# Moving loads, grouping the tails of two norms, and lending one weighting to POOL in a four-layer graph network kernel

## The chip, the cores and the metric

The kernel runs on one NeuronCore of a Trainium2 chip. The core has five engines with a queue each: PE (TensorE, matmuls; its weight loads are listed as PEld), DVE (VectorE), ACT (ScalarE), POOL (GpSimd) and SP (SyncE, which here only issues transfers). Engines execute their queues in order and wait for each other through semaphores. Transfers run on 16 DMA engines that all queues share. The metric is the device time of one execution in microseconds (us). Before the change three runs gave 7698.37, 7705.21 and 7706.85 us; the median is 7705.21.

## What is computed

A stack of four graph layers over 6250 nodes with 128 features and 100000 edges, sorted by their target `dst`. Each layer works on `h = relu(layernorm(x))` and adds its result to `x`. Shortened from the reference:

```python
# layer 0: attention summed into the source nodes, one softmax over all edges
h = h @ W_w + W_b
e = leaky_relu(h[src] @ a_src + h[dst] @ a_dst + a_b, 0.01)
out = segment_sum(softmax(e, axis=0) * h[dst], src)
# layer 1: message network, mean over dst, node network
m = relu(concat(h[src], edge_attr) @ W1a + b1a) @ W1b + b1b
agg = segment_sum(m, dst) / clip(count(dst), 1)
out = relu(concat(h, agg, u[0]) @ W2a + b2a) @ W2b + b2b
# layer 2: two graph attentions, four heads and one, each with batch norm and PReLU
h1 = prelu(bn(gatv2(h, heads=4)), pa)
h2 = prelu(bn(gatv2(h1, heads=1)), pa)
out = h2 + h @ skipW + skipb
# layer 3: three edge convolutions
for conv in (in, hid, out):
    z = relu(concat(h[dst], h[src] - h[dst]) @ W1 + b1) @ W2 + b2
    h = segment_max(z, dst)      # 0 where a node has no edge; relu between
```

All in float32, except some masks and counts in bfloat16.

## The kernel before

**Tiles.** Nodes are padded to 49 tiles of 128 (NT), edges to 782 tiles of 128 (TR), which are worked on in 196 chunks of 512. `x` stays on the chip as one tile of 128 x 49 x 128. What edges read of nodes is written as a table to memory, and POOL fetches its rows by indirect transfers, 128 rows each (`gather`, L390): the tables are T1 for layer 1 (`g`), TL1 and TL2 for layer 2's two attentions (`gl`, both named by their buffers `TL` and `TLb`), TB for each edge convolution (`gb`, three times 782). Layer 0 goes the other way: POOL scatters rows by source node into `rows_d` (`scatter`, L1259), a region per part, four parts in all, which SP clears ahead with `clear_rows` (L261).

**Preamble** (L116 to L255). `x` is loaded on ScalarE's queue in seven transfers of 448 KB. The edge lists `d_i` (SP) and `s_i` (ScalarE) are turned by VectorE and TensorE into columns of one number per edge. Then a loop over edge tiles counts how many edges each source tile has: VectorE compares (`oh`, L230), TensorE sums (`pc`, L233). Inside that loop the generator `node_steps` (L279) advances by one step per round. Its first steps load layer 0's weights (`wx`, `bx`, `av`), clear the rows of part 0 and append two columns to the weights, products with `av` (L308, L309); each later step does one node tile: normalise, transpose, project with `wx` and add the bias as a one-row product (L338, L339), copy to `ev` and store in the table T0 (L347). At the end a flag decides between the fast program, which runs here, and a general one.

**Layer 0's last part** (L1464 to L1550). When the last scatter is through, the rows of the fourth part are read back seven node tiles at a time. For each node tile ScalarE weights the J = 4 rows of each partition (`weigh`, L1301), VectorE builds a one-hot matrix (`oq`, L1303), TensorE sums (L1490), and the tile goes on to the layer norm of layer 1 and into T1.

**Mean layer, attentions.** The mean layer ends with the last node tile's network and the tables TL1 and TR1 (L1732, L1733). `attentions` (L1766) begins with the load of the single number `pa` (L381) and its negation `npa` (L1786). Each attention ends in `norm` (L2068): batch norm and PReLU of four node tiles at a time into `z`, then `finish` for every single tile: `to_tables` (L2124) projects to the second attention's tables TL2 and TR2; `to_x` (L2137) transposes, adds to `x`, layer-normalises, transposes and projects to the tables TA and TB of the first edge convolution, as three steps in a pipeline over tiles.

**Edge convolutions** (L2191). Per chunk TensorE builds the first layer's sum from TA and TB, ScalarE rectifies it (`z`, L2256), TensorE applies the second layer, VectorE scans for the running maximum. The first layer's bias is in the table TA by way of a row `bab` that `finish` (L2294) and `to_x` add.

**Order.** The Python code gives each engine's instructions; a scheduler sets their order per queue, so that an operation can stand earlier or later in its engine's queue than its line suggests.

Of the kernel before, what the change touches and what calls it, by code (L numbers as in the profile page):

```python
# [88 lines left out]
def tile_gnn_stack(ctx: ExitStack, tc: tile.TileContext, a: dict, out: bass.AP):  # L89
# [32 lines left out]
    xr = a["x"].rearrange("(i p) f -> p i f", p=P)  # L122
    for i in range(0, NT, 7):
        nc.scalar.dma_start(x[:, i:i + 7, :], xr[:, i:i + 7, :])
# [7 lines left out]
    with ExitStack() as st:  # L132
# [3 lines left out]
        node = node_steps(nc, tc, a, sh, st)  # L136
        d_i = one.tile([R, 1024], I32, name="d_i")
        nc.sync.dma_start(d_i, a["dst"].rearrange("(r j) -> r j", j=1024))
        s_i = one.tile([R, 1024], I32, name="s_i")
        nc.scalar.dma_start(s_i, a["src"].rearrange("(r j) -> r j", j=1024))  # L140
        edge_i = one.tile([R, 2], I32, name="edge_i")
# [137 lines left out]
def node_steps(nc, tc, a, sh, st):  # L279
# [3 lines left out]
    x, ident, ones = sh["x"], sh["ident"], sh["ones"]  # L283
# [3 lines left out]

    wx = one.tile([P, D + 2], F32, name="wx")
    bx = one.tile([1, D + 2], F32, name="bx")
    nc.scalar.dma_start(wx[:, :D], a["L0_gnn_W_w"])  # L290
    b0 = a["L0_gnn_W_b"]
    nc.scalar.dma_start(bx[:, :D], bass.AP(tensor=b0.tensor, offset=b0.offset, ap=[[0, 1], [1, D]]))
# [11 lines left out]
    clear_rows(nc, sh["rows_d"][0], none, 0)  # L304
    for j, av in enumerate(avs):
        for t, n in ((wx, P), (bx, 1)):
            pr = one.tile([n, D], F32, name=f"pr{n}")
            V.tensor_tensor(pr, t[:, :D], av[:n, :], OP.mult)  # L308
            V.tensor_reduce(t[:, D + j:D + j + 1], pr, AX.X, OP.add)  # L309
# [26 lines left out]
    def project(i):  # L336
        pp = ps.tile([P, D + 2], F32, name="np")
        nc.tensor.matmul(pp, live.pop(i), wx, start=True, stop=False)  # L338
        nc.tensor.matmul(pp, ones[0:1, :], bx, start=False, stop=True)  # L339
        live[i] = pp  # L340

    def keep(i):
        pp = live.pop(i)
        ev = w.tile([P, D + 1], F32, name="ev", bufs=4)
        S.copy(ev, pp[:, :D + 1])
        S.copy(sh["s_tab"][:, i:i + 1], pp[:, D + 1:])
        nc.sync.dma_start(sh["T0"][i * P:(i + 1) * P, :], ev)  # L347

    for i in range(NT + 2):
        if i < NT:  # L350
            norm(i)
        yield
        if 0 <= i - 1 < NT:
            project(i - 1)
        if 0 <= i - 2 < NT:
            keep(i - 2)
        yield
# [849 lines left out]
def attention_sum(ctx, tc, a, x, hT, T1, sh, ln_relu, transposed, bcast_row):  # L1207
# [89 lines left out]
    def weigh(w, rb, ew, J, row, bufs):  # L1297

        wt = w.tile([P, J, D], F32, name=f"wt{J}", bufs=bufs)
        for j in range(J):  # L1300
            S.activation(wt[:, j, :], rb[:, j, :D], AF.Copy, scale=ew[:, j:j + 1])  # L1301
# [182 lines left out]
    def total(b):  # L1484
        g, i = divmod(b, 7)
        ew, mv = accs[g]
        wt, oq = weigh(w, groups[g][:, i, :, :], ew[:, i, :], J, bank[:, P + 8:], 2)
# [278 lines left out]
def attentions(ctx, tc, a, x, TL1, TR1, TA, TB, sh, bcast_row, column, gather):  # L1766
# [17 lines left out]
    pa = bcast_row(cst, a["L2_gnn_pa"], 1, "pa")  # L1784
    npa = cst.tile([P, 1], F32, name="npa")
    V.tensor_scalar(npa, pa, -1.0, None, op0=OP.mult)  # L1786
# [281 lines left out]
    def norm(se, one, yT, stats, name, blocks, gam, bet, finish):  # L2068
# [14 lines left out]
        else:  # L2083
            eps = own.tile([P, 1], F32, name="leps")
            V.memset(eps, LN_EPS)
            wts.update(zip(("wab", "bab"), edge_weights(nc, own, a, "in")), eps=eps)
# [21 lines left out]
        for i0 in range(0, NT, 4):  # L2108
# [12 lines left out]
            for j in range(n):  # L2121
                finish(w, ps, i0 + j, z[:, :, j * P:(j + 1) * P])

    def to_tables(w, ps, i, z):  # L2124
        pp = ps.tile([P, 2 * D], F32, name="pp")
        for b in range(2):
            nc.tensor.matmul(pp, z[:, b, :], wts["wlr"][:, b, :], start=b == 0, stop=b == 1)
        ev = w.tile([P, 2, D + 1], F32, name="ev", bufs=4)
        V.tensor_tensor(ev[:, :, :D], pp.rearrange("p (s f) -> p s f", s=2),
                        wts["blr"].rearrange("p (s f) -> p s f", s=2), OP.add)  # L2130
        V.memset(ev[:, 0, D:], 1.0)
        nc.sync.dma_start(TL2[i * P:(i + 1) * P, :], ev[:, 0, :])
        nc.sync.dma_start(TR2[i * P:(i + 1) * P, :], ev[:, 1, :D])
# [3 lines left out]
    def to_x(w, ps, i, z):  # L2137
        n = slice(i * P, (i + 1) * P)
        it = {}

        def add():
            pp = ps.tile([P, P], F32, name="px")
            nc.tensor.transpose(pp, z[:, 0, :], ident)
            V.tensor_tensor(x[:, i, :], x[:, i, :], pp, OP.add)
            it["h"] = layer_norm(nc, w, x[:, i, :], wts["eps"])

        def turn():
            pp = ps.tile([P, P], F32, name="ph")
            nc.tensor.transpose(pp, it["h"], ident)
            it["hT"] = w.tile([P, P], F32, name="hT")  # L2150
            S.copy(it["hT"], pp)

        def tables():
            pp = ps.tile([P, 2 * D], F32, name="pp")
            nc.tensor.matmul(pp, it["hT"], wts["wab"], start=True, stop=True)
            ev = w.tile([P, 2 * D], F32, name="ev", bufs=4)
            V.tensor_tensor(ev, pp, wts["bab"], OP.add)  # L2157
            nc.sync.dma_start(TA[n, :], ev[:, :D])
            nc.sync.dma_start(TB[n, :], ev[:, D:])

        steps.append((add, turn, tables))
        for j in range(3):
            if i - j >= 0:
                steps[i - j][j]()
            if i == NT - 1:
                for m in range(j):
                    steps[i - m][j]()
# [7 lines left out]
def edge_weights(nc, pool, a, nm):  # L2175
# [7 lines left out]
    bab = pool.tile([P, 2 * D], F32, name=f"bab_{nm}")  # L2183
    V.memset(bab[:, D:], 0.0)
    b1 = a[f"L3_gnn_b1_{nm}"]
    nc.sync.dma_start(bab[:, :D], bass.AP(tensor=b1.tensor, offset=b1.offset, ap=[[0, P], [1, D]]))
    return wab, bab
# [3 lines left out]
def edge_convs(ctx, tc, a, x, TA0, TB0, hrow_d, sh, column, gather):  # L2191
# [21 lines left out]
    wab, bab, wo, bo = [None], [None], [], []  # L2213
# [154 lines left out]
```

## Time and profile before

| what | value |
|---|---|
| median of three runs | 7705.21 us |
| profiled execution | 7696.22 us |
| its span, first to last instruction | 7694.4 us |
| mean granted TensorE clock | 0.902 |
| busy: PE, DVE, ACT, POOL | 80%, 64%, 27%, 69% |
| indirect transfers on POOL: rows_d, g, gl (TL), gl (TLb), gb | 782 x 0.993, 782 x 0.947, 782 x 0.965, 782 x 1.002, 2346 x 0.957 us |

How to read it. The page shows the span in 40 slices of about 192 us; a digit is the busy share of a slice in tenths. Groups are instructions of one line, engine and shape with their busy time, the mean of one in ns, and the idle time of the engine before them with what ended it. In the timeline a line is: start, length, engine, line, operation, output<-input, and in brackets the idle time before and what ended it; a Q behind the engine's name marks the issue of transfers. From the timeline the stages are: preamble to about 172 us, layer 0's scattering parts to about 1204, its last part to 1322, mean layer to 2343, first attention to 3472 and its norm to 3537, second attention to about 4595 and its norm to 4674, edge convolutions to 7680, storing the output to 7694.

### The profile page before, as it was taken

To read this page: it belongs to the slowest core of one execution; us is meant where nothing else is said; L and a number is where in the kernel's file an instruction comes from. 1 tells how busy PE (TensorE), PEld (TensorE's weight loads), DVE (VectorE), ACT (ScalarE), POOL (GpSimd) and SP (SyncE) were. 2 spreads that over 40 slices of the span, in tenths; PEclk is the share of its full clock that TensorE was granted. 3 is DMA by queue.
4 is the path that set the end of the run, shared out by engine and by line. 5 is a ranking of instruction groups with operands and counts; after the bars stand their busy time and mean duration, and the time that the engine had idled before them with its cause. 6 is when DMAs were issued, how large, how long until landed. Compare 5 with 4: busy or idle time off the path is not lost.

```text
span 7694.4 us, 109942 instructions
## 1 busy us (share of the span) xinstructions
PE 6191.9 (80%) x35616; PEld 4418.6 (57%) x35616; DVE 4916.1 (64%) x15100; ACT 2115.0 (27%) x5081; POOL 5303.9 (69%) x5487
## 2 busy tenths in 40 slices
PE   6778886777777999996777777878778887777877
PEld 4677875555555666664554544555555555555554
DVE  5677886444446999995666666555555555555555
ACT  2134556222222222222111123222222222222222
POOL 0777772777776666654777755777767777677776
PEclk7778997999998999998888889999989999899999
DMA  3855763333336455433333324444434444333333
GB/s 121 258 162 168 216 189 124 93 92 93 92 87 133 142 144 146 143 104 95 88 89 93 89 79 125 122 126 122 126 114 123 125 122 126 110 119 118 117 118 108
DMA packets 778747, 954.40 MB, mean 124 GB/s; under 512 B 232584, under 2 KB 552494, under 8 KB 777942
## 3 DMA queue, kind: packets, MB, share of 16 engines
q1 hardware_dynamic: 555332, 519.06, 23.3%
q0 software_dynamic: 187680, 411.54, 18.5%
q10 hardware_dynamic: 35154, 16.67, 0.8%
q8 instruction: 289, 4.73, 0.3%
q14 instruction: 292, 2.39, 0.1%
HBM read 809.79 MB, written 137.02 MB: 123 GB/s over the span
## 4 chain that ended last, share of the span: by engine, by line
PE 39%; DMA 25%; POOL 13%; issue 9%; DVE 9%; ACT 2%; SPq 0%; POOLq 0%; DVEq 0%; ACTq 0%
DMA gb<-TB,srcE 13%; POOL gb L391 6%; PE pa L2011 5%; PE pz L2263 5%; DMA gl<-TLb,srcE 4%; PE pa L2290 4%; DMA g<-T,srcE 3%; PE pm L1892 3%; POOL gl L391 3%; DMA rows_d<-rw,pos 3%; PE pt L2251 3%; POOL g L391 3%; PE pb L2276 2%; PE pt L2253 2%; PE bank L1409 2%
## 5 line engine op out<-in xcount | busy, mean ns | idle before, releaser
L391 POOL DMA_INDIRECT gb<-TB,srcE x2346 | 2246.1, 957 | 859.6 <-issue 650.5
L2265 DVE TENSOR_TENSOR_SCAN sc<-mk,sc,pz 128x512 f32<-128x512 bf16 x585 | 748.4, 1279 | 1123.2 <-PE pz L2263 1123.2
L391 POOL DMA_INDIRECT gl<-TLb,srcE x782 | 783.5, 1002 | 364.4 <-issue 183.2
L391 POOL DMA_INDIRECT gl<-TL,srcE x782 | 754.4, 965 | 360.7 <-issue 153.8
L391 POOL DMA_INDIRECT g<-T,srcE x782 | 740.8, 947 | 357.5 <-issue 165.8
L2253 PE MATMUL pt<-ident,gb 128*128 128x128 f32 x2346 | 487.2, 295 | 608.0 <-DMA gb<-TB,srcE 597.3
L1259 POOL DMA_INDIRECT rows_d<-rw,pos x782 | 776.8, 993 | 251.8 <-issue 174.1
L2253 PEld LDWEIGHTS pt<-ident,gb 128*128 128x128 f32 x2346 | 315.2, 142 | 1051.8 <-DMA gb<-TB,srcE 772.9
L2256 ACT ACTIVATE z<-pt 128x512 f32<-128x512 f32 (+1 forms) x588 | 350.4, 596 | 1678.8 <-PE pt L2253 1571.3
L1897 ACT COPY mT<-pm 128x512 f32<-128x512 f32 (+1 forms) x588 | 343.7, 585 | 1399.0 <-PE pm L1894 1279.5
L1894 PEld LDWEIGHTS pm<-ident,gl 128*128 128x128 f32 x2346 | 317.9, 148 | 634.6 <-issue 318.2
L1892 PE MATMUL pm<-oh,wr 128*128 128x512 f32 (+1 forms) x1176 | 655.7, 641 | 31.6 <-DMA oh<-in_edge_weight 16.1
L2263 PE MATMUL pz<-z,wo 128*128 128x512 f32 (+1 forms) x1176 | 670.4, 655 | 0.0
L2290 PE MATMUL pa<-en,row 128*128 128x128 f32 x4692 | 669.0, 289 | 0.0
L2290 PEld LDWEIGHTS pa<-en,row 128*128 128x128 f32 x4692 | 624.2, 207 | 0.1
L1894 PE MATMUL pm<-ident,gl 128*128 128x128 f32 x2346 | 429.0, 290 | 239.9 <-DMA gl<-TLb,srcE 238.8
L2251 PE MATMUL pt<-oh,wr 128*128 128x512 f32 (+1 forms) x1176 | 612.5, 603 | 0.5 <-DVE ev L2157 0.5
L1898 DVE SCALAR_TENSOR_TENSOR lT<-mT,pm 128x512 f32<-128x512 f32 (+1 forms) x588 | 390.7, 675 | 286.1 <-ACT mT L1897 276.7
L2282 DVE TENSOR_SCALAR en<-iof,endE 128x128 f32<-128x128 f32 x2346 | 550.1, 301 | 0.0
L2276 PEld LDWEIGHTS pb<-ident,sc 128*128 128x128 f32 x2346 | 324.6, 153 | 357.9 <-issue 355.8
L2278 ACT COPY row<-pb 128x512 f32<-128x512 f32 (+1 forms) x588 | 344.1, 585 | 503.9 <-PE pb L2276 502.9
L2011 PE MATMUL pa<-px,oe 128*128 128x260 f32 x1564 | 407.7, 400 | 17.5 <-ACT px L2002 17.5
(346 smaller groups left out, 11735.5 us busy)
## 6 DMA issues: line engine op xcount, KB each, us to landing
mk<-mk_d SPq DMA_DIRECT2D x192, 1024.0 KB
mk<-mk_d SPq DMA_DIRECT2D x96, 512.0 KB
rows<-rows_d SPq DMA_DIRECT2D x98, 390.0 KB
gb<-TB,srcE POOLq DMA_INDIRECT x2346
wr<-TA SPq DMA_DIRECT2D x141, 256.0 KB
rows_d<-none SPq DMA_DIRECT2D x3, 9360.0 KB
ea<-in_edge_attr SPq DMA_DIRECT2D x195, 128.0 KB
wr<-TR SPq DMA_DIRECT2D x47, 448.0 KB
```

The costliest lines, as they stand in the source:

```text
L391: nc.gpsimd.indirect_dma_start(out=dst, out_offset=None, in_=table, in_offset=bass.IndirectOffsetOnAxis(ap=idx, axis=0),)
L1259: ins = nc.gpsimd.indirect_dma_start(out=rows_d[s], out_offset=bass.IndirectOffsetOnAxis(ap=idx, axis=0), in_=src, in_offset=None)
L1892: nc.tensor.matmul(pm[:, c0 * P:], wr[:, fb], oh[:, c0 * P:], start=True, stop=False)
L1894: nc.tensor.matmul(pm[:, c * P:(c + 1) * P], gl[:, c, fb], ident, start=False, stop=c == 3, is_transpose=True)
L2011: nc.tensor.matmul(pg, oe[:, c, :], px[:, c, :], start=c == c0, stop=c == 3)
L2251: nc.tensor.matmul(pt[:, c0 * P:], wr, oh[:, c0 * P:], start=True, stop=False)
L2253: nc.tensor.matmul(pt[:, c * P:(c + 1) * P], gb[:, c, :], ident, start=False, stop=c == 3, is_transpose=True)
L2263: nc.tensor.matmul(pz[:, c0:], wo[conv], z[:, c0:], start=True, stop=True)
L2265: V.tensor_tensor_scan(sc[:, c0:], masks.pop(k)[1][:, c0:], pz[:, c0:], 0.0 if carry[0] is None else carry[0][:, 511:512], OP.add, OP.max)
L2276: nc.tensor.transpose(pb[:, c, :], sc[:, c * P:(c + 1) * P], ident)
L2282: V.tensor_scalar(en[:, c, :], iof, endE[:, t:t + 1], None, op0=OP.is_equal)
L2290: nc.tensor.matmul(pa, row[:, c, :], en[:, c, :], start=c == c0, stop=c == 3)
```

## The change

- The loads of `x` go from ahead of the preamble to behind the load of `s_i` on the same queue. `pa` is loaded and negated at the preamble's start.
- `clear_rows` of part 0 is called in the fifteenth node step, not in the second. (In the compiled order of SP's queue the large transfer of the clearing stands where it stood; the small one has moved behind four T0 stores.)
- Layer 0's bias is loaded to all 128 partitions and added by VectorE when a projected tile leaves PSUM; the one-row product and ScalarE's copy go.
- In layer 0's last part one of the four weightings of a node tile is done by POOL, and `wt` and `oq` have three buffers instead of two.
- `to_tables` stores two node tiles per transfer. `to_x` takes four node tiles per pipeline step: one root, one reciprocal and one copy for four, table copies of two tiles alternately on ScalarE and VectorE, without bias, and two tiles per store.
- The edge convolutions' first bias goes from the table into the rectify, as one number per partition; `bab` goes, and `finish` copies on ScalarE.

```diff
@@ preamble
     x = const.tile([P, NT, D], F32, name="x")
-    xr = a["x"].rearrange("(i p) f -> p i f", p=P)
-    for i in range(0, NT, 7):
-        nc.scalar.dma_start(x[:, i:i + 7, :], xr[:, i:i + 7, :])
...
         node = node_steps(nc, tc, a, sh, st)
+        npa = const.tile([P, 1], F32, name="npa")
+        pa = a["L2_gnn_pa"]
+        nc.scalar.dma_start(npa, bass.AP(tensor=pa.tensor, offset=pa.offset, ap=[[0, P], [1, 1]]))
+        V.tensor_scalar(npa, npa, -1.0, None, op0=OP.mult)
+        sh["npa"] = npa
...
         nc.scalar.dma_start(s_i, a["src"].rearrange("(r j) -> r j", j=1024))
+        xr = a["x"].rearrange("(i p) f -> p i f", p=P)
+        for i in range(0, NT, 7):
+            nc.scalar.dma_start(x[:, i:i + 7, :], xr[:, i:i + 7, :])
@@ node_steps
-    bx = one.tile([1, D + 2], F32, name="bx")
+    bx = one.tile([P, D + 2], F32, name="bx")
...
     yield
-    clear_rows(nc, sh["rows_d"][0], none, 0)
     for j, av in enumerate(avs):
-        for t, n in ((wx, P), (bx, 1)):
-            pr = one.tile([n, D], F32, name=f"pr{n}")
-            V.tensor_tensor(pr, t[:, :D], av[:n, :], OP.mult)
+        for t in (wx, bx):
+            pr = one.tile([P, D], F32, name="pr")
+            V.tensor_tensor(pr, t[:, :D], av, OP.mult)
...
-        nc.tensor.matmul(pp, live.pop(i), wx, start=True, stop=False)
-        nc.tensor.matmul(pp, ones[0:1, :], bx, start=False, stop=True)
+        nc.tensor.matmul(pp, live.pop(i), wx, start=True, stop=True)
...
-        ev = w.tile([P, D + 1], F32, name="ev", bufs=4)
-        S.copy(ev, pp[:, :D + 1])
-        S.copy(sh["s_tab"][:, i:i + 1], pp[:, D + 1:])
-        nc.sync.dma_start(sh["T0"][i * P:(i + 1) * P, :], ev)
+        ev = w.tile([P, D + 2], F32, name="ev", bufs=4)
+        V.tensor_tensor(ev, pp, bx, OP.add)
+        S.copy(sh["s_tab"][:, i:i + 1], ev[:, D + 1:])
+        nc.sync.dma_start(sh["T0"][i * P:(i + 1) * P, :], ev[:, :D + 1])
...
+        if i == 14:
+            clear_rows(nc, sh["rows_d"][0], none, 0)
@@ weigh, layer 0's last part
         for j in range(J):
-            S.activation(wt[:, j, :], rb[:, j, :D], AF.Copy, scale=ew[:, j:j + 1])
+            if j < helped:
+                nc.gpsimd.tensor_scalar(wt[:, j, :], rb[:, j, :D], ew[:, j:j + 1], None, op0=OP.mult)
+            else:
+                S.activation(wt[:, j, :], rb[:, j, :D], AF.Copy, scale=ew[:, j:j + 1])
...
-        wt, oq = weigh(w, groups[g][:, i, :, :], ew[:, i, :], J, bank[:, P + 8:], 2)
+        wt, oq = weigh(w, groups[g][:, i, :, :], ew[:, i, :], J, bank[:, P + 8:], 3, 1)
@@ attentions
-    pa = bcast_row(cst, a["L2_gnn_pa"], 1, "pa")
-    npa = cst.tile([P, 1], F32, name="npa")
-    V.tensor_scalar(npa, pa, -1.0, None, op0=OP.mult)
+    npa = sh["npa"]
...
+    def to_tables(w, ps, i0, n, z):
+        for q0 in range(0, n, 2):
+            m = min(2, n - q0)
+            ev = w.tile([P, 2, 2, D + 1], F32, name="ev")
...
+            store(TL2, i0 + q0, m, ev[:, :m, 0, :])
+            store(TR2, i0 + q0, m, ev[:, :m, 1, :D])
...
+        def add():
+            pp = ps.tile([P, 4, P], F32, name="px")
+            mv = w.tile([P, 4, 2], F32, name="mv")
             for j in range(n):
+                nc.tensor.transpose(pp[:, j, :], z[:, 0, j * P:(j + 1) * P], ident)
+            for j in range(n):
+                xi = x[:, i0 + j, :]
+                V.tensor_tensor(xi, xi, pp[:, j, :], OP.add)
...
+            S.activation(r[:, :n, 0], mv[:, :n, 1], AF.Sqrt, bias=wts["eps"], scale=1.0)
+            V.reciprocal(r[:, :n, 0], r[:, :n, 0])
...
+            S.copy(it["hT"][:, :n, :], pp[:, :n, :])
...
+                (V.tensor_copy if q0 else S.copy)(ev[:, :m, :], pp[:, :m, :])
+                store(TA, i0 + q0, m, ev[:, :m, :D])
+                store(TB, i0 + q0, m, ev[:, :m, D:])
@@ edge_convs
-            S.activation(z[:, c0 * P:], pt[:, c0 * P:], AF.Relu)
+            S.activation(z[:, c0 * P:], pt[:, c0 * P:], AF.Relu, bias=b1[conv], scale=1.0)
...
-                V.tensor_tensor(ev, pp, bab[conv + 1], OP.add)
+                S.copy(ev, pp)
```

## Prediction

> **What bounds the kernel now.** I read the page's slices, groups and chain first, then the waits of the first 175 us, then the start and end of each stage in the timeline, then windows inside the stretches that the change touches.
>
> ```profile
> POOL 0777772777776666654777755777767777677776
> PEclk7778997999998999998888889999989999899999
> PE 39%; DMA 25%; POOL 13%; issue 9%; DVE 9%; ACT 2%; SPq 0%; POOLq 0%; DVEq 0%; ACTq 0%
> L391 POOL DMA_INDIRECT gb<-TB,srcE x2346 | 2246.1, 957 | 859.6 <-issue 650.5
> L1259 POOL DMA_INDIRECT rows_d<-rw,pos x782 | 776.8, 993 | 251.8 <-issue 174.1
> ```
>
> Three quarters of the span are indirect transfers that POOL issues one by one: busy 0.95 to 1.0 us each and about 0.3 us of issue behind it, some 1.26 us apiece. No line of the change touches these stages' rate. What it touches are the stretches where the POOL row falls: the preamble (0 to 172 us), the last part of layer 0 (1204 to 1323), the turn from the mean layer to the attention (about 2343), and the two norm tails (3480 to 3537, 4600 to 4674). POOL restarts after each, so microseconds saved there move everything behind them.
>
> ```profile
> 5.95 0.40 SPq L265 DMA_DIRECT2D rows_d<-none  x1
> 17.03 4.50 ACTq L140 DMA_DIRECT2D s_i<-in_src  x1
> 41.37 0.82 ACTq L297 DMA_DIRECT2D av<-in_L_gnn_a_w  x2
> 32.20 0.69 DVE L186 TENSOR_SCALAR slo<-s_i 98x1024 int32<-98x1024 int32 x1 [12.37 <-DMA s_i<-in_src]
> 44.40 0.29 DVE L308 TENSOR_TENSOR pr<-wx,av 128x128 f32<-128x128 f32 x1 [9.60 <-DMA av<-in_L_gnn_a_w]
> 54.20 0.55 DVE L230 TENSOR_TENSOR oh<-iob,hi 128x392 bf16<-128x392 bf16 x1
> ```
>
> The preamble's timeline: VectorE is held 12.37 us for `s_i` and 9.60 us for `av`; the first count comparison starts at 54.20. Then, in windows of PE, PEld, DVE, ACT, POOL (busy, instructions), PEclk, DMA share and GB/s:
>
> ```profile
> 80.00:100.00 20.00, 19.97 (x65) 13.40 (x65) 9.22 (x31) 8.89 (x41) 0.00 (x0) 0.50 0.15 41
> 1247.45:1263.67 16.22, 13.23 (x79) 12.24 (x78) 11.97 (x45) 15.43 (x47) 0.00 (x0) 0.79 0.44 144
> 4640.00:4660.00 20.00, 15.94 (x62) 8.62 (x62) 18.14 (x97) 15.99 (x51) 0.00 (x0) 1.00 0.37 105
> ```
>
> The counting phase is full on TensorE, the last part of layer 0 on ScalarE, the second norm tail on VectorE and ScalarE together. At the turn to the attention:
>
> ```profile
> 2334.53 0.15 DVE L1786 TENSOR_SCALAR npa<-pa 128x1 f32<-128x1 f32 x1 [10.29 <-DMA pa<-in_L_gnn_pa]
> 2334.61 0.28 DVE L1715 TENSOR_TENSOR x<-x,pn 128x128 f32<-128x128 f32 x1
> 2343.44 0.94 POOL L391 DMA_INDIRECT gl<-TL,srcE  x1 [42.41 <-DMA TR<-ev]
> ```
>
> A one-number load stands in VectorE's queue ahead of the last tile's work.
>
> **The change part by part** (A to F).
>
> *A, preamble, start.* `s_i` now goes ahead of the seven `x` loads on ScalarE's queue, so the 12.37 us wait goes. What is late next is `av`. Its two loads stay last on that queue, behind `x`, `wx` and a `bx` that is now 64 KB. Before, `av` was issued at 41.37, just as the DMA engines came to the end of the 9360 KB clear: this clear, 3.2 MB of `x` and some 0.8 MB more at the 383 to 386 GB/s of the 10 to 30 us windows are 35 us from 5.95 on. I take it that the load waited for the clear's completion counter. In the changed program's order the large clear still stands right behind the first small stores on SP's queue; only its 195 KB remainder sits behind four T0 stores. And `bx` waits for the eighth counter, as `av` did, so `av` follows about 41.4 + 0.4 and lands near 44.8. The product `pr<-wx,av` stands in VectorE's order ahead of the first comparison, which so starts near 45 instead of 54.2: 9 us saved. Ends: nothing, if the bytes land later; 19 us, if `av` is not held (start near 35, when the other VectorE work is through).
>
> *A, preamble, counting and projecting, 54 to 168 us.* Out of TensorE go 49 bias products, x98 records in 114 us with 38.4 us of 137.3 us of overlapping matmul records, or 0.73 us each in the timeline: some 31 to 36 us. ScalarE loses 49 copies of 0.268. VectorE gains 49 adds of 128x130 from PSUM; the row nearest in shape is the add `x<-x,px` with 0.266: 13 us. VectorE's sum in the phase was comparisons 50.6, statistics 11.2 + 7.4, counts 2.3 and about 5 of small ones, 77; it becomes 90. TensorE falls from 111 to about 78. So VectorE becomes the bound. It also waited 27.3 us for TensorE's counts, and now waits for each projection in order, with comparisons queued behind it and TensorE waiting for these. I take 95 us for the 114: 19 saved. Ends: 0, if all 27 us of waiting stay beside the 90; 28, if VectorE is full. A together: −28, between −5 and −45.
>
> The Trainium skill (TensorE: Matmul & The Clock Gate, Part 1: The HAM clock gate) says the array gets its full clock after a few us of sustained work. Here the granted clock reads 0.50 from 80 to 180 us with TensorE 97% busy, so row and rule differ; by the rule the removed products would weigh about half, and A would save some 15 us less on TensorE, which VectorE's sum makes the smaller term anyway.
>
> *B, last part of layer 0.* Seven tiles take 16.22 us, and ScalarE is busy for 15.43 of them. Each tile has four weightings L1301; three ACT weightings instead of four save one of about 0.293 (its spacing in the timeline), 49 of them 14.4 us. TensorE (13.2 of 16.2 us) and VectorE (12.0) are next, so seven tiles cannot fall much under 14.2. On POOL, idle from 1202.7 to 1322.2, the weighting has no row in this trace; other POOL work on 128x128 takes 0.20 (memset), 0.23 (iota) and 0.88 us (affine select), all under the 1.71 us of a tile now. Order: the 49 stand behind the last scatter and ahead of the first gather of the mean layer, which wait for nothing else there; TensorE's first product of each tile now waits for POOL, with a third buffer for cover. I take −9, of 14.4 at most, as TensorE and VectorE come close; ends −14 and +3 (POOL's replies late every tile).
>
> The Trainium skill (GPSIMD Engine Reference, section 1. Specifications) gives GpSimd an SBUF interface shared with VectorE, with contention when VectorE reads two SBUF inputs. The rows that this rule bears on are L1303 (24.4 us of a 75 us window) and L1497 (12.3), which do that half the time; no POOL arithmetic lies beside them in this trace. By the rule VectorE could lose the POOL time, seven times 0.23 to 0.88: 13.6 to 18.2 us per seven tiles, which makes B anything from −9 to +14.
>
> *C, `pa` load.* It leaves SP's queue at 2322.08 and VectorE's at 2334.53. The add behind it had its TensorE result at 2324.8, so all of the last tile, its store and the first gather move by 2334.6 − 2324.9 = 9.7. In the preamble it costs ScalarE's queue one issue of about 0.4, and `npa` stands in VectorE's order ahead of the first use of `d_i`, where VectorE had 3.69 us of waiting for `x` until now: 0. Take −9.7 (−8 to −10.5).
>
> *D, first norm tail.* 98 stores become 50. TensorE ends its 196 products at 3528.59 with 2.2 us of waiting for `ev`; then SP still has six stores of a backlog until 3534.26, and the gather follows at 3536.92. With half the stores the queue keeps up (0.32 + 0.43 us per pair of tiles against 1.8 of TensorE): end of TensorE near 3526.4, add 0.42, two issues 0.75, the same 2.66 to the gather: 3530.4. −6.5 (−3 to −9).
>
> *E, second norm tail.* 73.1 us from 4600.47 to the gather at 4673.61. VectorE loses 49 adds of 0.42 and 36 each of two small operations (0.155, 0.145), and gets 12 copies of about 0.59: from 0.9 to near 0.55 of the time. ScalarE is what remains: its records from 4600 to 4664 sum to 66.6 (normalise 21.6, roots 13.0, copies 11.7, rectify 20.3); roots fall to 3.9, copies to 7.6, the new table copies add 7.6, so 61. That saves 5.6 us; steps of four tiles cost about as much at fill and drain as single ones, since the last group is one tile. −5 (−10 to +4).
>
> *F, edge convolutions.* The bias rides in the rectify that exists (L2256, 0.596 us x588; ScalarE 20 to 30% busy there), a column load takes the place of a row load, the add of `finish` goes from VectorE to ScalarE. All beside gathers at 1.26 us; nothing reaches POOL. Were this cover gone, 588 biases at 0.2 (0.49 for a scaled, biased 128x128 against 0.27 for a copy) would be 118 us. 0 (−3 to +5).
>
> Sum: −28 − 9 − 9.7 − 6.5 − 5 + 0 = −58. The profiled run's 7696 gives 7638; it stands 9 us under the median 7705, against which I forecast **7647**.
>
> **The rivals.**
> 1. *VectorE takes the preamble's gain.* Adds and comparisons in one queue wait for TensorE in turn, and the phase stays at about 110 us: A −12, total −42: 7663. For it: 27.3 us of VectorE waits there; against it: TensorE loses a quarter of its work.
> 2. *The moved loads do what they say*: `av` not behind the clear, first comparison near 35, VectorE full: A −45, total −75: 7630. Against it: issue order and 41.37.
> 3. *B gives nothing or costs a few us*, because POOL and VectorE hold each other up: −49 to −45: 7656 to 7660.
> 4. *Slower: POOL's weighting bounds layer 0's last part.* If one takes t, the 49 take 49t against 98 us now. The other parts' 49 us are eaten at t = 3.0 us, and slower by 0.2% (15 us; less can't be told from no change here) begins at 3.3; at 4 us the time is 7754. Against it: 0.20 to 0.88 us.
>
> **How the numbers follow.** Chances: forecast 0.50, rival 1 0.20, rival 2 0.10, rival 3 0.10, several small terms together under 15 us 0.05, rival 4 0.05. The bounds of all terms together reach −84 and −8; 8 in 10 lie between −88 (rival 2 with B, D and E at their ends) and −22 (rivals 1 and 3 together, D at its end and E at nothing): 7617 to 7683. Rivals 1 to 3 all are faster by over 0.2%, as 42 us are 0.5%. So faster 0.89, same 0.06, slower 0.05.
>
> **What would show it.** A: first comparison near 45, wait for `s_i` gone, a wait for `av` left, large clear still issued near 6 us, VectorE fuller than TensorE from 60 us on, first masks read near 144 instead of 172. B: ScalarE still full, seven tiles in 14.5 to 15 us, POOL weightings under 1 us. C: no wait at L1786. D: SP's last store within 2 us of TensorE's end. E: 68 us. F: the same 20.2 us for 16 gathers. Wrong if POOL's weightings take over 2 us, if the counting phase keeps 110 us, or if a load that was early before (`x` for the statistics) is late now.

## The result, and the profile after

The changed kernel takes 7650.22 us (median of four runs, 7641.85 to 7651.46) against 7703.94 for the kernel before (four runs): a ratio of 0.9929, 95% interval 0.9916 to 0.9941. The forecast was 7647, with a range of 7617 to 7683. A second set of runs of both gave 7641.99 against 7695.99, ratio 0.9929 (0.9913 to 0.9946). The profiled execution took 7649.58 us, its span is 7647.8 us, 46.6 less than before.

The total was met, its terms were not. POOL's transfers cut the span into stages: each begins or ends with the start of a first or last scatter or gather. The table has the starts' differences in us; "control" is the second profile of the changed kernel.

| stage (prediction's step) | before | after | difference | control |
|---|---|---|---|---|
| start to first scatter (A) | 186.9 | 149.5 | −37.4 | 151.6 |
| first to last scatter | 1014.8 | 1023.0 | +8.2 | 1025.2 |
| last scatter to first gather of the mean layer (B) | 120.4 | 110.3 | −10.1 | 108.5 |
| its gathers | 977.9 | 979.9 | +2.0 | 979.1 |
| to the first gather of the attention (C) | 43.4 | 38.0 | −5.4 | 39.9 |
| first attention's gathers | 1071.7 | 1070.5 | −1.2 | 1071.6 |
| first norm tail (D) | 121.8 | 117.0 | −4.8 | 112.9 |
| second attention's gathers | 1025.6 | 1029.1 | +3.5 | 1025.3 |
| second norm tail (E) | 111.0 | 97.5 | −13.5 | 99.6 |
| first edge convolution's gathers (F) | 985.7 | 992.2 | +6.5 | 992.1 |
| the rest (F) | 2035.1 | 2040.7 | +5.6 | 2033.6 |

The stages which no kernel of this study touches spread between the profiles of the chips where the kernel before takes about 7700 us: the mean layer's gathers from 977.9 to 980.7 us, the second attention's from 1025.3 to 1033.5. So a single difference of a few us says little, unless a row of the trace carries it.

The page of the changed kernel (slices, chain and groups):

```profile
POOL 1777774777767667645777746777767777677776
PEclk8688997999999999998888888999999999899999
PE 27%; DMA 15%; POOL 12%; issue 9%; DVE 6%; ACT 1%; SPq 0%; POOLq 0%; DVEq 0%; ACTq 0%
L395 POOL DMA_INDIRECT gb<-TB,srcE x2346 | 2256.5, 962 | 845.6 <-issue 677.0
L1263 POOL DMA_INDIRECT rows_d<-rw,pos x782 | 784.4, 1003 | 250.1 <-issue 170.7
```

The bound is what it was, but two groups are dearer: the scatters, 993 to 1003 ns each, and the `gb` gathers, 957 to 962. The scatters are told below, and so is one of the gathers, which alone makes 2.4 of the 5 ns; the other kernels' `gb` means spread from 955 to 963 without an order that this study can name. The preamble's timeline of the changed kernel:

```profile
6.77 0.40 SPq L270 DMA_DIRECT2D rows_d<-none  x1
1.16 0.66 ACTq L142 DMA_DIRECT2D s_i<-in_src  x1
43.49 0.93 ACTq L301 DMA_DIRECT2D av<-in_L_gnn_a_w  x2
47.18 0.29 DVE L311 TENSOR_TENSOR pr<-wx,av 128x128 f32<-128x128 f32 x1 [17.68 <-DMA av<-in_L_gnn_a_w]
47.40 0.56 DVE L235 TENSOR_TENSOR oh<-iob,hi 128x392 bf16<-128x392 bf16 x1
```

`s_i` is early and its wait is gone. VectorE is through with the edge columns at about 29.5 and then stands 17.68 us for `av`. The large clear still goes out at 6.77. Windows of the changed kernel, in the counting phase, in layer 0's last part and in the second norm tail:

```profile
80.00:100.00 20.00, 13.95 (x60) 7.65 (x60) 18.22 (x71) 8.69 (x35) 0.00 (x0) 0.82 0.14 40
1206.20:1222.40 16.20, 13.28 (x105) 11.83 (x104) 14.89 (x57) 16.03 (x50) 5.40 (x9) 1.00 0.63 203
4580.00:4600.00 20.00, 16.70 (x82) 11.79 (x81) 16.24 (x72) 19.70 (x45) 0.00 (x0) 1.00 0.50 141
```

Columns are PE, PEld, DVE, ACT, POOL, then the granted clock. The counting phase has gone from TensorE (19.97 of 20 us) to VectorE (18.22). The window of the last part is on ScalarE still, with VectorE close (14.89 of 16.2). That of the second tail is now on ScalarE alone (19.70 of 20).

### The profile page after: what moved, and what is told of

Read it like the earlier page. It is cut to its first block, busy times and chain, and to the rows that moved or that the text cites. A ratio compares the mean times of both kernels' runs of the same rounds, so it can differ in the third digit from the quotient of the medians.

```text
span 7647.8 us, 108692 instructions
## 1 busy us (share of the span) xinstructions
PE 6123.7 (80%) x35518; PEld 4370.9 (57%) x35518; DVE 4879.2 (64%) x14915; ACT 2174.3 (28%) x5020; POOL 5358.7 (70%) x5536
## 4 chain that ended last, share of the span: by engine, by line
PE 27%; DMA 15%; POOL 12%; issue 9%; DVE 6%; ACT 1%; SPq 0%; POOLq 0%; DVEq 0%; ACTq 0%
DMA gb<-TB,srcE 10%; POOL gb L395 8%; PE pa L2016 5%; PE pz L2291 4%; POOL gl L395 4%; PE pa L2318 4%; DMA gl<-TLb,srcE 4%; PE pm L1897 3%; PE pt L2279 3%; PE pb L2304 2%; PE pt L2281 2%; PE pm L1899 2%; DVE px L2003 1%; PE sp L1921 1%; DVE y L2024 1%
## 5 line engine op out<-in xcount | busy, mean ns | idle before, releaser
L1263 POOL DMA_INDIRECT rows_d<-rw,pos x782 | 784.4, 1003 | 250.1 <-issue 170.7
L2284 ACT ACTIVATE z<-pt,b 128x512 f32<-128x512 f32 (+1 forms) x588 | 403.5, 686 | 1537.4 <-PE pt L2281 1519.2
```

The lines of the kernel that those rows point to most:

```text
L1263: ins = nc.gpsimd.indirect_dma_start(out=rows_d[s], out_offset=bass.IndirectOffsetOnAxis(ap=idx, axis=0), in_=src, in_offset=None)
```

## The experiments

The first four ran on a chip where the kernel before takes 9185 us. POOL waits longer between its transfers there (the mean layer's gathers take 1222 to 1230 us instead of 978); why is not known. Their times and stages are compared among themselves and with the kernel before on that chip. No run of the unmodified changed kernel exists there. The others ran where before takes 7696 to 7710.

### No weighting on POOL

```diff
-        wt, oq = weigh(w, groups[g][:, i, :, :], ew[:, i, :], J, bank[:, P + 8:], 3, 1)
+        wt, oq = weigh(w, groups[g][:, i, :, :], ew[:, i, :], J, bank[:, P + 8:], 3, 0)
```

> The changed kernel with all four weightings on ScalarE again, the third buffers kept. Theory (ScalarE bounded layer 0's last part, and POOL's share is worth a weighting per tile): from the last scatter to the first gather of the mean layer it goes back from 109.3 us towards the 119.5 us of before; 118 to 121 us there, and the whole near 7659, 9 us over the changed kernel's 7650. Rival a (the third buffers did it, not POOL): about 110 us there and 7650. Rival b (POOL's weightings hold VectorE up, and it is nearly full at 15 of 16.2 us): under 109 us there and faster than 7650. The 782 scatters before it, 1016 us before and 1024 us after the change, are to show whether they depend on the change at all.

Measured: 9134.26 us, ratio to before 0.9947 (0.9925 to 0.9969). Last scatter to first gather 123.0 us, against 110.8 and 111.5 in the two kernels below that keep POOL's part on the same chip, and 121.4 in the one made from before. So the weighting is worth 12 us in its place and the third buffers nothing: theory, with a bit more than expected. The whole could not be compared with the changed kernel there. What stood out was in another stage: a scatter took 982 ns on average, as in the kernel made from before (983), and 994 and 992 in the two that keep POOL's part. The stage as a whole does not follow this on this chip: first to last scatter took 1335.5 us here and 1332.7 and 1318.8 in those two, 1317.9 in the one made from before. What sets it there is open, so that a longer scatter makes a longer stage is shown only by the runs on the faster chips below.

### Layer 0's bias back on TensorE

```diff
...
-        nc.tensor.matmul(pp, live.pop(i), wx, start=True, stop=True)
+        nc.tensor.matmul(pp, live.pop(i), wx, start=True, stop=False)
+        nc.tensor.matmul(pp, ones[0:1, :], bx[0:1, :], start=False, stop=True)
...
-        V.tensor_tensor(ev, pp, bx, OP.add)
-        S.copy(sh["s_tab"][:, i:i + 1], ev[:, D + 1:])
+        S.copy(ev[:, :D + 1], pp[:, :D + 1])
+        S.copy(sh["s_tab"][:, i:i + 1], pp[:, D + 1:])
```

> The changed kernel with layer 0's bias again as a one-row product on TensorE and the copy out of PSUM on ScalarE; the loads keep their new order. Theory (the products were what the counting phase waited for): the phase from the first comparison to the end of the preamble goes back from 91 to near 119 us, the first scatter from 149.5 to about 178 us, granted clock 0.50 in the phase, the whole near 7678. Rival (the phase is shorter because the edge columns were ready early and VectorE had less in it): no more than 10 us longer, near 7658.

Measured: 9143.28 us, ratio 0.9950 (0.9931 to 0.9969). The first scatter is at 179.8, against 150.1 and 150.3 in the kernels around it that have the bias on VectorE, and 183.7 in the one made from before. So of the preamble's gain some 29.5 us are the bias's way (the products on TensorE) and only about 4 the order of the loads. The window and groups of this kernel's counting phase:

```profile
80.00:100.00 20.00, 19.37 (x62) 12.38 (x62) 11.53 (x37) 9.21 (x39) 0.00 (x0) 0.50 0.12 34
```

```profile
L235 DVE TENSOR_TENSOR oh<-iob,hi 128x392 bf16<-128x392 bf16 (+1 forms) x98 | 50.7, 556 | 25.6 <-PE pc L238 25.6
L342 PE MATMUL np<-bx,ones 1*128 1x130 f32 x98 | 37.5, 482 | 0.0
```

TensorE is full again at a granted clock of 0.50, and VectorE waits 25.6 us for its counts. In the changed kernel, without the products, the clock reads 0.74 to 0.92 from 60 to 140 us, and VectorE's comparisons wait for no count. The same groups of the kernel before, then of the changed kernel:

```profile
L230 DVE TENSOR_TENSOR oh<-iob,hi 128x392 bf16<-128x392 bf16 (+1 forms) x98 | 50.6, 553 | 27.4 <-PE pc L233 27.3
```

```profile
L235 DVE TENSOR_TENSOR oh<-iob,hi 128x392 bf16<-128x392 bf16 (+1 forms) x98 | 51.0, 551 | 0.0
L347 DVE TENSOR_TENSOR ev<-np,bx 128x130 f32<-128x130 f32 x49 | 13.8, 286 | 8.2 <-PE np L341 8.0
```

### Only the load of `pa` moved

```diff
@@ kernel before
...
-    pa = bcast_row(cst, a["L2_gnn_pa"], 1, "pa")
-    npa = cst.tile([P, 1], F32, name="npa")
-    V.tensor_scalar(npa, pa, -1.0, None, op0=OP.mult)
+    npa = sh["npa"]        # loaded and negated in the preamble, as in the changed kernel
```

> The kernel before with the load of pa moved to the preamble and nothing else. The prediction's step: 9.7 us less between the last gather of the mean layer and the first of the attention, 43.4 to 33.7, the whole near 7694. Theory now: the load was slow because the 12.2 KB store of hrow, 6250 numbers of 2 bytes, occupies all DMA engines for some 20 us at 1 GB/s; the store of the last table rows that comes next is held by the same, so only about 5 us, 43.4 to 38, the whole near 7699.

Measured: 9186.61 against 9185.38, ratio 1.0003 (0.9993 to 1.0013): no gain that can be seen. The step's 9.7 us would be a ratio of 0.9989, outside the interval; the theory's 5 us, 0.9995, lie in it. The turn takes 52.6 us here; without a profile of before on this chip that figure decides nothing by itself.

### `hrow` stored in rows

```diff
-    nc.sync.dma_start(hrow_d.rearrange("(i p) -> p i", p=P), has)
+    hf = one.tile([P, NT], F32, name="hasf")
+    V.tensor_copy(hf, has)
+    hp = ps.tile([P, P], F32, name="pn")
+    nc.tensor.transpose(hp[:NT, :], hf, ident)
+    hb = one.tile([NT, P], BF, name="hasb")
+    V.tensor_copy(hb, hp[:NT, :])
+    nc.sync.dma_start(hrow_d.rearrange("(i p) -> i p", p=P), hb)
```

> The changed kernel with hrow turned on TensorE and stored as 49 rows of 256 bytes instead of 6272 single numbers. Theory (the store of single numbers clogs the DMA engines at the turn to the attention): the engines' share near nothing there instead of full, the last table store lands in about 2 us instead of 6.6, the SP queue no longer held for 9.7 us; last gather to first gather 38.0 to 31 or 33 us, the whole near 7644. Rival (the clog comes from something else, such as the table stores themselves): 38 us and 7650.

Measured: 9117.63 us, ratio 0.9916 (0.9884 to 0.9947), the lowest median of the four, though the intervals overlap. First the changed kernel as it is, its SP timeline and a window at the turn:

```profile
2271.31 0.37 SPq L1769 DMA_DIRECT2D hrow_d<-has  x1
2274.91 9.74 SPq L1739 DMA_DIRECT2D TL<-ev  x1
2293.58 0.42 SPq L1740 DMA_DIRECT2D TR<-ev  x1
2300.79 0.94 POOL L395 DMA_INDIRECT gl<-TL,srcE  x1 [37.08 <-issue]
```

```profile
2285.00:2290.00 5.00, 1.69 (x6) 0.72 (x4) 2.56 (x9) 0.79 (x2) 0.00 (x0) 0.84 1.60 13
```

Soon after this 12.2 KB store goes out the 16 DMA engines are counted as more than full (share 1.60 in the window) and move 13 GB/s. The last table store, issued at 2293.58, lets POOL go only at 2300.79. With rows instead of single numbers:

```profile
2862.09 0.43 SPq L1740 DMA_DIRECT2D TR<-ev  x1
2862.74 0.32 SPq L1775 DMA_DIRECT2D hrow_d<-hasb  x1
2864.34 0.95 POOL L395 DMA_INDIRECT gl<-TL,srcE  x1 [47.30 <-DMA hrow_d<-hasb]
```

From the table store to the gather it is 2.3 us instead of 7.2. The store also stands behind the last table store now, no longer ahead of it; the trace's packet records tell form from place. In the changed kernel the store is 6272 packets of 2 bytes, from 2272.2 to 2289.8 us, and they take 369 us of the engines' time together; the tables' packets of 1024 bytes behind them take 239 ns each. Here it is 49 packets of 256 bytes that take 0.9 us together, and the tables' packets take 49 ns.

The turn was expected at 31 to 33 us, 5 to 7 less than in the changed kernel, and took 48.2, against 51.2 and 54.5 on this chip: 3 and 6 us less. On a faster chip it became 34.8 (last experiments), against 38.0 to 41.7 in the kernels with single numbers.

### The changed kernel again, and layer 0's weights ahead of `x`

The changed kernel as it is:

> The changed kernel once more, as the control for the runs sent with it. Theory (the change acts in the stretches where POOL stands still): against the kernel before on the same chip 45 to 60 us less, preamble 36 to 38 us shorter, the first gather of the first edge convolution again at 6.57 us of POOL time. On a chip with slower long stages, where the scatters of layer 0 take 1318 us behind a late preamble and 1333 to 1336 behind an early one, the scatter stage again gives some 15 us back; if that was chance, it gives nothing.

Measured: 7641.99 us, 54.0 under before; its stages are the table's last column. The first gather of the first edge convolution takes 6.57 us again, and the scatter stage again some 8 us more than before although this chip is the fast one.

```diff
+        next(node)               # wx, bx, av are issued here
         xr = a["x"].rearrange("(i p) f -> p i f", p=P)
         for i in range(0, NT, 7):
             nc.scalar.dma_start(x[:, i:i + 7, :], xr[:, i:i + 7, :])
```

> The changed kernel with layer 0's weights (wx, bx, av) loaded ahead of x on ScalarE's queue. Theory (av is late only because it waits behind the 9360 KB clear, and VectorE's order has its product ahead of the first comparison): the wait of 17.7 us for av goes, the first comparison starts at 29 to 31 instead of 47.4, the first scatter at 131 to 135 instead of 149.5, the whole 10 to 18 us under the changed kernel. Rival (the counting phase is then held by x, which loads later): the wait moves to the first statistics, first scatter no earlier than 145.

Measured: 7640.32 us, ratio 0.9925 (0.9908 to 0.9941), 1.7 under the control, whose four runs spread over 11 us; the gain cannot be seen in the whole. In its place it can. Timeline of this kernel:

```profile
7.14 36.00 ACTq L146 DMA_DIRECT2D x<-in_x  x7
27.24 0.28 DVE L312 TENSOR_TENSOR pr<-wx,av 128x128 f32<-128x128 f32 x1
27.45 0.56 DVE L236 TENSOR_TENSOR oh<-iob,hi 128x392 bf16<-128x392 bf16 x1
43.17 1.28 ACT L323 ACT_TABLE_LOAD   x1 [43.17 <-DMA x<-in_x]
44.91 0.52 DVE L236 TENSOR_TENSOR oh<-iob,hi 128x392 bf16<-128x392 bf16 x1
```

The wait for `av` is gone and the first comparison starts at 27.45. But the seven `x` loads now hold ScalarE's queue until 43.2, as the last of them waits for the clear in turn (it was issued at 42.76, when the clear's last part reported, at 42.7); the first root stands behind them, VectorE waits for that root, and its comparisons go on at 44.91. First scatter 140.9 instead of 151.6: 10.7 us, between theory (131 to 135) and rival (145 or later), and both mechanisms are there.

### Only the convolutions' bias moved

```diff
@@ kernel before
-            S.activation(z[:, c0 * P:], pt[:, c0 * P:], AF.Relu)
+            S.activation(z[:, c0 * P:], pt[:, c0 * P:], AF.Relu, bias=b1[conv], scale=1.0)
...
-                V.tensor_tensor(ev, pp, bab[conv + 1], OP.add)
+                S.copy(ev, pp)
```

> The kernel before with the edge convolutions' bias moved into the rectify, the row loads gone and the copy of finish on ScalarE; nothing else. The prediction's step: nothing beside the gathers, within 5 us. Theory now: the rectify grows from 0.596 to 0.686 us without a cost, each convolution within 1 us of before; the 5.6 us that the first gather of the changed kernel loses belong to the order at the second norm tail and do not show here, the first gather takes 0.94 to 1.0. Rival: the column loads or the bias bring the loss, the first gather takes 6.57 us and the whole is 5 to 10 us over before.

Measured: 7701.82 against 7695.99, ratio 1.0007 (0.9997 to 1.0016); the gathers of the three convolutions 985.5, 987.0 and 983.8 us (before 985.7, 985.9, 985.8), the first gather 0.94. The rectify grew from 596 to 687 ns and nobody waits for it. The add of `to_x` became a copy in this kernel, too. The prediction's nothing holds for this edit.

### The clearing of `agg` in pieces

```diff
-    V.memset(aggs[0], 0.0)
+    for i in range(0, NP, 224):
+        V.memset(aggs[0][:, i:i + 224], 0.0)
```

> The changed kernel with the clearing of agg (one VectorE memset of 128 x 6272, 5.29 us) cut into 28 memsets of 128 x 224. Theory (POOL cannot work on the first gather while that one memset holds the SBUF interface that both share: 0.32 us ahead of it, 5.29 in it, 0.95 behind it are 6.56, and 6.57 was measured): the first gather takes under 2 us, the first convolution starts 4 to 6 us earlier, the whole 4 to 5 us less. Rival (the gather waits for transfers): still 6.57 us or near it, no gain.

Measured: 7639.75 us, ratio 0.9927 (0.9911 to 0.9944), not to be told from the control in the whole. Timelines of the changed kernel and of this one:

```profile
4614.84 6.57 POOL L395 DMA_INDIRECT gb<-TB,srcE  x1 [96.53 <-issue]
4615.16 5.29 DVE L2237 MEMSET agg<- 128x6272 f32 x1 [4.08 <-issue]
4621.71 0.95 POOL L395 DMA_INDIRECT gb<-TB,srcE  x1 [0.30 <-issue]
```

```profile
4615.12 6.74 DVE L2238 MEMSET agg<- 128x224 f32 x28 [2.83 <-DMA TB<-ev]
4616.06 0.94 POOL L395 DMA_INDIRECT gb<-TB,srcE  x1 [94.05 <-issue]
4617.30 0.94 POOL L395 DMA_INDIRECT gb<-TB,srcE  x1 [0.30 <-issue]
```

The 6.57 us are gone, and the first convolution's gathers take 984.6 instead of 992 (988.5 and 988.7 in the two kernels below that have this edit among others). That the one long memset held the gather fits in length, 0.32 + 5.29 + 0.96. But in the kernel before four gathers went by beside the same memset:

```profile
4673.61 0.94 POOL L391 DMA_INDIRECT gb<-TB,srcE  x1 [109.54 <-issue]
4674.12 5.29 DVE L2209 MEMSET agg<- 128x6272 f32 x1 [2.12 <-issue]
4674.86 0.94 POOL L391 DMA_INDIRECT gb<-TB,srcE  x1 [0.31 <-issue]
```

So cutting it is shown to help where it hurt, with 6.56 or 6.57 us in six profiles of the changed kernel's order with the memset uncut, and 0.94 in three with it cut; what decides whether the memset holds a gather stays open. It is not the offset alone: held was a gather that had run for 0.32 us, not held one that had run for 0.51 us in the kernel before, and one that had run for 0.18 to 0.20 us, the second of the stage, in the four other kernels made from before.

### All three edits, with and without POOL's weighting

```diff
+        next(node)                                   # ahead of the loads of x
...
-    nc.sync.dma_start(hrow_d.rearrange("(i p) -> p i", p=P), has)
+    nc.sync.dma_start(hrow_d.rearrange("(i p) -> i p", p=P), hb)
...
-    V.memset(aggs[0], 0.0)
+        V.memset(aggs[0][:, i:i + 224], 0.0)
```

> The changed kernel with three edits that were run singly: layer 0's weights loaded ahead of x, hrow stored in rows, the clearing of agg in 28 pieces. From their own places 10.7 us, 4 to 6 us and 5.6 us, so about 20 us under the changed kernel: 61 to 75 us under the kernel before on the same chip, a ratio of 0.990 to 0.992 on a chip where before takes 7700. Rival (such gains at the stretches do not add up, as the first of them did not show in the whole): a ratio of 0.9925 as for the changed kernel itself.

Measured: 7627.38 us (7622.53 to 7634.62), ratio 0.9900 (0.9884 to 0.9915), 76 under before on the same chip and better than the changed kernel's 0.9929: the three edits were worth some 20 us together, though two of them were within the noise alone. First scatter 140.8, turn 34.8, first gather 0.94.

```diff
-        wt, oq = weigh(w, groups[g][:, i, :, :], ew[:, i, :], J, bank[:, P + 8:], 3, 1)
+        wt, oq = weigh(w, groups[g][:, i, :, :], ew[:, i, :], J, bank[:, P + 8:], 3, 0)
```

> The same with all weightings on ScalarE. Theory (a program with the POOL weighting pays 10 ns in each of the 782 scatters, typical 0.970 us in six such profiles against 0.960 in four without, so 8 us, for 10 to 12 us in layer 0's last part): scatters at 0.960, scatter stage 1015 to 1017 instead of 1023 to 1025, last part 120 instead of 110, the whole 2 to 4 us over the kernel with it, which can hardly be told apart. Rival (the 10 ns come from the preamble's change or the chip): scatters at 0.970 and the whole 10 us over.

Measured: 7636.61 us, ratio 0.9911 (0.9897 to 0.9924). Scatter stage 1015.4 against 1023.0 with POOL's weighting, last part 125.3 against 112.9: the expected 8 us back, and 12.4 instead of 10 lost. The medians differ by 9 us, more than the 4.8 that the two stages leave, but the intervals overlap, so a net gain of POOL's weighting is not shown.

### POOL's weighting alone, and once

```diff
@@ kernel before
-        wt, oq = weigh(w, groups[g][:, i, :, :], ew[:, i, :], J, bank[:, P + 8:], 2)
+        wt, oq = weigh(w, groups[g][:, i, :, :], ew[:, i, :], J, bank[:, P + 8:], 3, 1)
```

> The kernel before with one weighting of four on POOL in layer 0's last part, three buffers, and nothing else. The prediction's step: 9 us less. Theory now: 10 us less in the last part (120.4 to 110), but the scatters ahead of it take 0.970 instead of 0.960 us each, 8 us more, so 7693 to 7697 where before takes 7696, a ratio within 0.0005 of 1. Rival (the scatters' 10 ns belong to other parts of the change): scatters at 0.960, 9 to 10 us less.

Measured: 7699.39 against 7703.59, ratio 0.9995 (0.9986 to 1.0005). The groups of this kernel:

```profile
L1259 POOL DMA_INDIRECT rows_d<-rw,pos x782 | 786.4, 1006 | 252.8 <-issue 173.1 <-DVE rw L1389 19.8 <-ACT wt L1304 12.8
L1302 POOL TENSOR_SCALAR wt<-rows,ew 128x128 f32<-128x128 f32 x49 | 29.8, 609 | 61.9 <-PE pa L1493 24.5 <-ACT ew L1483 10.6 <-ACT wt L1304 9.9
```

Last part 108.0 instead of 120.4, scatter stage 1024.5 instead of 1014.8. Of the 12.4 us of one stage 9.7 are paid in the stage ahead of it.

```diff
+        wt, oq = weigh(w, groups[g][:, i, :, :], ew[:, i, :], J, bank[:, P + 8:], 3, 1 if b == 0 else 0)
```

> The kernel before with one single weighting on POOL, that of the first node tile, and nothing else. Theory (it is enough that the program holds such an instruction, since all scatters come before the first of them): scatters typically 0.970 us, scatter stage 1023 to 1025 on a chip where before takes 7700, last part 120. Rival (the cost goes with the number of weightings, by whatever they leave behind for the next execution): 0.960.

Measured, one run of each on a third chip: 7726.64 us beside 7709.76 for before, too few to compare. Scatter stage 1023.8, last part 123.2. Its group and three neighbouring scatters of its timeline, then three of the kernel before:

```profile
L1302 POOL TENSOR_SCALAR wt<-rows,ew 128x128 f32<-128x128 f32 x1 | 0.6, 609 | 9.7 <-ACT ew L1483 9.7
```

```profile
900.12 0.97 POOL L1259 DMA_INDIRECT rows_d<-rw,pos  x1 [0.30 <-issue]
901.40 0.97 POOL L1259 DMA_INDIRECT rows_d<-rw,pos  x1 [0.30 <-issue]
902.67 0.97 POOL L1259 DMA_INDIRECT rows_d<-rw,pos  x1 [0.30 <-issue]
```

```profile
899.72 0.96 POOL L1259 DMA_INDIRECT rows_d<-rw,pos  x1 [0.30 <-issue]
900.98 0.96 POOL L1259 DMA_INDIRECT rows_d<-rw,pos  x1 [0.30 <-issue]
902.24 0.96 POOL L1259 DMA_INDIRECT rows_d<-rw,pos  x1 [0.30 <-issue]
```

One such instruction in the program, executed once and after all scatters, makes a typical scatter 0.97 instead of 0.96 us: a median of 971 ns against 958, of which some 3 may be the chip's, as the gathers take 947 ns here against 944. The third buffers, which came with it, do not: the two kernels that have them without POOL's weighting stand at 961 and 958 ns.

## Why the prediction was right, point by point

**Total.** Right: −54 measured at the medians, −58 forecast against the median. That it came so near is partly luck. In their places A, B and E gave more than forecast (−37.4, −10.1 and −13.5 for −28, −9 and −5), C and D less (−5.4 and −4.8 for −9.7 and −6.5), together −71 for −58. Two costs that were not in the sum took most of the difference back, 8.2 us in the scatters and 5.6 in one gather. (The ends of the terms add up to −91.5 and −4, not to −84 and −8; the range does not rest on them.)

**A, start.** Right as a mechanism: the load of `av` stayed behind the clear (`bx` ahead of it was issued at 43.11, when the clear's last part reported, at 43.1), the first comparison came at 47.4 (forecast 45), and `s_i` no longer counts. It was worth 6.8 us, not 9. Rival 2 would have needed another order of the loads: with the weights ahead of `x` the preamble is 10.7 us shorter still.

**A, counting.** The term was mis-sized: 114 to 95 was forecast, −19. First comparison to the first POOL instruction behind the preamble went from 119.4 (54.2 to 173.6) to 91.1 us (47.4 to 138.5), −28, its own far end. The failed step is that VectorE would keep part of its 27.3 us of waiting for TensorE's counts: it kept none, and waits 8.0 us for projections in their place. Rival 1 said it would keep nearly all and is out.

On the clock the Trainium skill (TensorE: Matmul & The Clock Gate, Part 1: The HAM clock gate) would have the busier TensorE at the full clock; here the phase that filled TensorE read 1.00 from 60 to 80 us, as the page has it, and then 0.50 up to 180 us, though TensorE was busy for 97% of the time up to 160; the phase that leaves it a fifth to a third free reads 0.74 to 0.92. After these first 20 us the measurement differs from the page.

**B.** Right in place (−10.1; −9 was forecast), and wrong as a whole. The step priced the weighting by what it does in its own stretch, 0.61 us of POOL under a tile's time; but a typical scatter became some 10 ns longer by the instruction's presence in the program, +8 us over 782 of them, and alone the edit gives nothing measurable (0.9995). No step of the sum had that. Rival 3 had the outcome, that B gives nothing, but by another cause. The step also set the time of a tile at 1.71 us; the profile's 16.22 us per seven are 2.3, and so rival 4's 98 us for 49 tiles should be 113.

For the rule that was weighed there (the Trainium skill, GPSIMD Engine Reference, section 1. Specifications), the prediction named two rows, and one does not fit: `oq` compares with a row of `bank`, which lies in PSUM, so only L1497 of the kernel before, `x<-acc,rs,x`, reads SBUF twice. In the changed kernel 29 of these 49 lie beside a weighting and take 335 ns, the other 20 take 341, as all did before; POOL's weightings take 618 ns beside them and 604 elsewhere. So VectorE shows no loss, and rival 3's cause is out.

**C.** Wrong step: "all of the last tile, its store and the first gather move by 9.7". What the load waited for was not its own. The store of `hrow`, 6272 numbers of 2 bytes, keeps the DMA engines busy for 17.6 us, and the table rows that queue behind it are slow for some 6 us more. Once the load is away the last table store meets the same: −5.4 in the profile.

**D.** Mechanism right, size smaller: from TensorE's first product of the tail to the gather 56.8 us became 52.0 (52.4 in the control), −4.8 and −4.3 where −6.5 was forecast. The control's −8.9 in the table holds 4.5 us from ahead of that product, where the change does nothing. TensorE's products end 45.6 us after they start instead of 48.4, the gather follows 6.4 us later instead of 8.3.

**E.** Mis-sized: −13.5 for −5. The windows from the first rectify to the gather, before and after:

```profile
4600.47:4673.61 73.14, 51.76 (x200) 29.04 (x200) 59.89 (x312) 59.42 (x173) 0.00 (x0) 0.94 0.43 130
4554.44:4614.84 60.40, 42.46 (x196) 30.29 (x196) 42.96 (x199) 52.41 (x114) 0.00 (x1) 0.90 0.56 169
```

The step counted what ScalarE would be relieved of, and that was nearly right: 59.4 us busy became 52.4, by 7.0 where 5.6 were forecast. It left out ScalarE's idle time, much of it waits for TensorE and VectorE: with VectorE down from 59.9 to 43.0 us it fell from 13.7 to 8.0, and the stretch from 73.1 to 60.4 us (62.9 in the control).

**F.** Right for the edit itself. What came on top is the first gather at 6.57 us, 5.6 us that belong to the memset of `agg` and the order of starts at that point; the prediction looked at the rate of the gathers, not at their first.

**Rival 4** (POOL bounds the last part) is out with 0.61 us per weighting.

## What to carry to other kernels

Price an instruction that is new to an engine in every stage where that engine is the bound, not only in the one where it runs. When a wait is removed, ask what made the awaited transfer slow, since the next transfer in the queue meets the same: a few KB in pieces of 2 bytes kept the DMA engines busy for 17.6 us, and turned into rows they took 0.9 us of one. Small gains at several places can lie within the noise one by one and be clear together, so read each in its own stage of the profile and run the sum.

## What the runs showed of the hardware that was not expected

- The scatter's line and its operands in the trace are the same in kernels with and without the POOL weighting. The nine profiles with it have medians of 969 to 972 ns per scatter, the five without 958 to 962. The gathers, typically 944 to 947 ns, show no such difference. Why is not settled.
- The store of 6272 single numbers of 2 bytes: share of the DMA engines from 1.1 to 2.05 from 2275 to 2295 us, at 1 to 50 GB/s.
- One VectorE memset of 5.29 us held a gather that had started 0.32 us ahead of it for its whole length; the same memset, begun 0.51 us into the gather in the kernel before, held none.
- The granted TensorE clock of the preamble's counting phase was lower with TensorE full from 80 to 100 us (0.50) than with 70% busy (0.82). Products that both kernels have took 420 ns each in the slower phase and 338 in the faster one (`np<-wx,h`), so the lower clock itself makes TensorE look busier, and which came first is not shown.
